# Column sums for a softmax: two column tiles of 64 with 512 columns, or four of 32 with 256

## The chip, the cores and the metric

The kernel runs on one core of one Trainium2 chip. Five engines work side by side there, each through its own list of instructions: TensorE (PE in the profile, with PEld for its weight loads), VectorE (DVE), ScalarE (ACT), GpSimd (POOL) and SyncE (SP), which here issues nearly all transfers. The metric is the time on the device in microseconds (us), lower is better; the time before is 1205.87 us, the median of three runs from 1204.80 to 1207.79.

## The reference

A block of a diffusion transformer: for two sequences of 1024 tokens with 256 features, all in float32, a layer norm, self-attention with 16 heads of 64, cross-attention to 77 tokens of context, a gated feed-forward, and then a second feed-forward with weights rounded to -1, 0, 1. The change touches the softmax of self-attention alone:

```python
def mha(xq, ctx, wq, wk, wv, wo, bo):
    b, sq, _ = xq.shape
    sk = ctx.shape[1]
    q = (xq @ wq).reshape(b, sq, H, DH).transpose(0, 2, 1, 3)
    k = (ctx @ wk).reshape(b, sk, H, DH).transpose(0, 2, 1, 3)
    v = (ctx @ wv).reshape(b, sk, H, DH).transpose(0, 2, 1, 3)
    scores = jnp.einsum('bhqd,bhkd->bhqk', q, k) / math.sqrt(DH)
    attn = jax.nn.softmax(scores, axis=-1)
    out = jnp.einsum('bhqk,bhkd->bhqd', attn, v)
    out = out.transpose(0, 2, 1, 3).reshape(b, sq, INNER)
    return out @ wo + bo
```

## The kernel before

Self-attention is cut into 32 units (NU = B * NP * 2): a unit is one sequence, one pair of heads and one half of the queries (512). Its scores are kept transposed, with keys on the 128 partitions and 2 x 512 queries of the two heads in the 1024 columns, in eight blocks of 128 keys (kb). So the softmax runs down the partitions: the maximum and the sum of a query are over partitions and over the eight blocks.

For each block, PE makes the scores in a tile of two PSUM banks (`scores`, L342, matmul L347), ACT copies them to SBUF (L927), and DVE keeps a running maximum (`running_max`, L357, L363). When the eight are done, DVE folds the maximum over the partitions (L366 to L385), a transfer writes it to DRAM and another spreads it to all partitions (`md`, `wide`, L386 and L387), and ACT places it in PSUM (`mb`, L391). Then each block is shifted by DVE (L400; one block by POOL, L395), exponentiated in place by ACT (L404), added on POOL into a running sum `pacc` (L411), and multiplied with the values on PE (`times_v`, L419).

The sums that the change rewrites come after this. `summed` (L448) lets PE multiply `pacc` by ones, which adds over the 128 partitions: `sums_by_ones` (L438) does it in two matmuls, one for each head, each of 512 columns, into the two halves of the partitions (two column tiles of 64; all 64 rows of a half hold the same numbers). The tile `tot` comes from the same two buffers of two banks each (`two_banks`, L53) as the scores. ACT copies it to SBUF as `rinv` (L454). `sums_packed` (L456) sends one row of each half to a row of 1024 in DRAM (`td`) and reads it back as 128 partitions of 8 numbers (`few`, L464). `inverted_packed` (L466) takes the reciprocal on DVE, writes it to DRAM and spreads it again over the 64 partitions of each half of `rinv` (L471). `normalised` (L480) multiplies the unit's output by it on POOL. The last two units take no part in the packing; their sums are inverted where they stand (`inverted`, L476), and the last unit's are added up block by block in PSUM (L969).

The order is written out by hand for PE, DVE, ACT and POOL (`manual_schedule`); SP's transfers are placed by the scheduler. The loop at L922 goes through slots, four to a unit (`q` = 0 to 3), two blocks in each. In a slot of unit u, PE does the two blocks of scores of u, then a piece of something else (projections, the product with wo, parts of cross-attention's weights; L281), and the values of older blocks, LAG = 7 slots behind. The sums of unit u - 3 stand at the end of slot q = 0 of unit u, their reciprocal at q = 1, the multiplication at q = 2. So on PE the sums are preceded by matmuls of the form 128 rows by 64 columns (L281 or L419) and followed by scores, which are 64 rows by 128 columns (L347).

Of the kernel before, what the change touches and what calls it, by code (L numbers as in the profile page):

```python
# [29 lines left out]
H, DH = 16, 64  # L30
# [13 lines left out]
def block_kernel(ctx: ExitStack, tc: tile.TileContext, a: dict, out: bass.AP):  # L44
    nc = tc.nc
    PSUM = bass.MemoryType.PSUM

    def g(name):
        return a["L0_" + name]
# [3 lines left out]
    def two_banks(name):  # L53
        return ps2.tile([P, 1024], FP, tag="s", name=name)
# [15 lines left out]
    ones = const.tile([P, P], FP, name="ones")  # L70
# [110 lines left out]
    NU = B * NP * 2  # L181
# [4 lines left out]
    with ExitStack() as sa:  # L186
# [9 lines left out]
        SQ = 32  # L196
        md = [dram.tile([1024], FP, name=f"md{u}") for u in range(NU)]
        td = [dram.tile([2, 1024], FP, name=f"td{u}") for u in range(NU)]
        sT, maccs, paccs, rinvs, tots, few = {}, {}, {}, {}, {}, {}
# [36 lines left out]
        for n in range(3):  # L236
            nc.scalar.dma_start(
                out=vec[4 * n : 4 * n + 4, :],
                in_=g(f"xcond_norm{n + 1}_b").rearrange("(o p) -> o p", p=P),
            )  # L240
        for c in range(DC):
            nc.scalar.dma_start(
                out=vec[28 + B * c : 28 + B * (c + 1), :],
                in_=a["cond_1024"][:, c * P : (c + 1) * P],
            )
        nc.scalar.dma_start(
            out=vec[12:28, :], in_=g("xcond_ff_b1").rearrange("(o p) -> o p", p=P)
# [190 lines left out]
        def sums_by_ones(tot, src, start, stop):  # L438
            for j in range(2):
                nc.tensor.matmul(  # L440
                    tot[j * DH : (j + 1) * DH, :512],
                    lhsT=ones[:, :DH],
                    rhs=src[:, j * 512 : (j + 1) * 512],
                    start=start,
                    stop=stop,
                )

        def summed(u):  # L448

            if u in paccs:  # L450
                tots[u] = two_banks("tot")
                sums_by_ones(tots[u], paccs.pop(u), True, True)
            rinvs[u] = p1.tile([P, 512], FP, tag="rinv", name="rinv")
            nc.scalar.copy(rinvs[u], tots.pop(u)[:, :512])  # L454

        def sums_packed(u):  # L456

            for j in range(2):
                nc.sync.dma_start(
                    out=td[u][0:1, j * 512 : (j + 1) * 512],  # L460
                    in_=rinvs[u][j * DH : j * DH + 1, :],
                )
            few[u] = small.tile([P, 8], FP, tag="few", name="few")
            nc.sync.dma_start(out=few[u], in_=td[u][0, :].rearrange("(p i) -> p i", i=8))  # L464

# [456 lines left out]
        for slot in range(NS + 12):  # L922
            u, q = slot // SLOTS, slot % SLOTS
# [4 lines left out]
            v, k = (slot - LAG + 1) // SLOTS, (slot - LAG + 1) % SLOTS  # L928
# [34 lines left out]
            w, k = (slot - LAG) // SLOTS, (slot - LAG) % SLOTS  # L963
# [9 lines left out]
            if slot == NS + 6:  # L973
                summed(NU - 1)
                for part in range(4):
                    inverted(NU - 1, part)
                normalised(NU - 1)
            elif q == 2 and 0 <= u - 3 < NU - 2:
                normalised(u - 3)
            elif slot == NS + 5:  # L980
                for part in range(4):
                    inverted(NU - 2, part)
                normalised(NU - 2)
            for job in extras.pop(slot, []):
                job[0](*job[1:])
            if slot in (NS + 7, NS + 8):
                n = slot - NS - 7
# [5 lines left out]
            if q == 0 and 0 <= u - 3 < NU - 1:  # L993
                summed(u - 3)
                if u - 3 < NU - 2:
                    sums_packed(u - 3)
# [41 lines left out]
        for name in ("w1", "w2"):  # L1038
# [4 lines left out]
            for i in range(2):  # L1043
                if name == "w1":
                    src = g("ffn_w1").rearrange("(c p) d -> p c d", p=P)[:, 4 * i : 4 * i + 4, :]
                    dst = raws[name][i].rearrange("p (c d) -> p c d", d=D)
                else:
                    src = g("ffn_w2")[i * P : (i + 1) * P, :]
# [173 lines left out]
    with (  # L1222
# [60 lines left out]
        for t in range(0, NT, 2):  # L1283
            i = t - TB
# [382 lines left out]
```

## Time and profile before

| What | Value |
|---|---|
| Median of three runs | 1205.87 us (1204.80 to 1207.79) |
| The profiled execution's own time | 1205.21 us |
| Its span, first to last instruction | 1203.4 us |
| Granted TensorE clock, mean over the span | 0.987 |
| Sums by ones, PE (L440) | 124 records of 592 ns |
| Copy of the sums, ACT (L454), 512 columns | 31, 585 ns in the middle |
| Scores' matmuls, PE (L347) | 1024 records, 258.1 us busy |
| Additions to pacc, POOL (L411) | 186 + 31, 2.37 us each |

The page of a profile gives busy time and counts of each engine over the span, the chain of work that ended last, and groups of instructions with the idle time before them and what ended it. A timeline lists instructions in order of time, those of one line merged: start, length, engine, line, operation, tiles written and read, shapes, number, and in brackets the idle time of the engine before it. For PE the shapes begin with rows*columns of the array that a matmul uses, and its lengths overlap, since matmuls are pipelined and their ends modelled: the time from start to start is the time that one takes. "A <- B" in a list of waits means that A's engine stood still until B was done; the numbers are total us, times, and the longest.

### The profile page before, as it was taken

The numbers are of one execution on the slowest core, as the hardware profiler recorded it, in microseconds if no ns is written. First come the engines' busy times: TensorE is split into PE (matmuls) and PEld (weight loads), VectorE is DVE, ScalarE is ACT, GpSimd is POOL, SyncE is SP. The second block draws the span as 40 slices with busy tenths as digits, with TensorE's granted clock in tenths as the row PEclk, the third lists the DMA queues.
The fourth block names the chain that finished last, engine by engine and source line by source line (L and its number), as shares of the span: only waits on it lengthen the run. The fifth ranks groups of instructions, "written<-read, shape, count | busy, mean of one in ns | idle before, by whom it ended". The sixth has DMA issues, their size and how long they took to land.

```text
span 1203.4 us, 16673 instructions
## 1 busy us (share of the span) xinstructions
PE 1166.8 (97%) x5885; PEld 576.5 (48%) x5885; DVE 946.1 (79%) x1398; ACT 814.6 (68%) x1032; POOL 809.6 (67%) x625
## 2 busy tenths in 40 slices
PE   8898999999999999999999999989999999999996
PEld 4342334334334343343433333346878766586684
DVE  4779789879888888988978988984767753568596
ACT  4788888888887887888889788751343341555365
POOL 5579888888888788879788989851425325433244
PEclk9999999999999999999999999999999999999996
DMA  7101212212122211311213112221020011000000
GB/s 229 36 30 42 76 53 64 69 52 68 45 78 60 64 56 54 88 33 54 65 48 108 58 45 88 77 65 36 1 66 20 1 62 35 1 18 10 9 10 27
DMA packets 65892, 63.23 MB, mean 53 GB/s; under 512 B 22875, under 2 KB 56149, under 8 KB 65297
## 3 DMA queue, kind: packets, MB, share of 16 engines
q1 hardware_dynamic: 65745, 62.15, 17.0%
q8 instruction: 46, 0.75, 0.3%
q14 instruction: 37, 0.30, 0.1%
q10 hardware_dynamic: 64, 0.02, 0.0%
HBM read 54.63 MB, written 7.52 MB: 52 GB/s over the span
## 4 chain that ended last, share of the span: by engine, by line
PE 81%; DVE 11%; ACT 4%; POOL 2%; issue 2%; DMA 0%; DVEq 0%; ACTq 0%; POOLq 0%
PE sc L347 16%; PE pav L419 16%; PE pp L281 9%; PE pu L1568 8%; PE sc L734 5%; PE po L801 5%; PE pv L281 4%; PE po L1594 4%; DVE macc L363 3%; DVE sT L400 3%; PE po L281 3%; PE tot L440 2%; ACT sT L927 2%; PE pu L1423 1%; PE po L1470 1%
## 5 line engine op out<-in xcount | busy, mean ns | idle before, releaser
L411 POOL TENSOR_TENSOR pacc<-pacc,sT 128x1024 f32<-128x1024 f32 x186 | 440.8, 2370 | 59.8 <-ACT sT L404 50.3
L363 DVE TENSOR_TENSOR macc<-macc,sc 128x1024 f32<-128x1024 f32 x192 | 233.8, 1218 | 77.7 <-ACT sT L927 66.1
L927 ACT COPY sT<-sc 128x1024 f32<-128x1024 f32 x256 | 247.5, 1015 | 51.4 <-PE sc L347 51.2
L404 ACT ACTIVATE sT<-sT 128x1024 f32<-128x1024 f32 x256 | 259.9, 1062 | 14.9 <-DVE sT L400 13.7
L347 PE MATMUL sc<-qT,kT 64*128 64x512 f32 x1024 | 258.1, 619 | 7.1 <-DVE macc L363 6.1
L400 DVE TENSOR_TENSOR sT<-sT,mb 128x1024 f32<-128x1024 f32 x225 | 261.8, 1206 | 2.8 <-ACT mb L391 2.8
L419 PE MATMUL pav<-sT,v 128*64 128x512 f32 x1024 | 250.0, 606 | 2.7 <-ACT sT L404 2.4
L347 PEld LDWEIGHTS sc<-qT,kT 64*128 64x128 f32 x1024 | 85.8, 185 | 158.3 <-DVE macc L363 60.5
L419 PEld LDWEIGHTS pav<-sT,v 128*64 128x64 f32 x1024 | 62.4, 136 | 151.1 <-issue 76.1
L1568 PE MATMUL pu<-h2T,ffw 128*128 128x512 f32 (+1 forms) x320 | 114.6, 509 | 0.0
L768 POOL TENSOR_TENSOR pr<-pr,t 128x616 f32<-128x616 f32 x32 | 39.2, 1225 | 104.1 <-DVE t L767 57.8
L411 POOL TENSOR_TENSOR pacc<-sT 128x1024 f32<-128x1024 f32 x31 | 73.8, 2381 | 46.0 <-ACT sT L404 46.0
L1568 PEld LDWEIGHTS pu<-h2T,ffw 128*128 128x128 f32 x320 | 59.5, 190 | 44.0 <-issue 39.9
L734 PE MATMUL sc<-G,h1T 128*128 128x308 f32 x256 | 74.0, 433 | 4.5 <-DVE pr L752 3.3
L801 PE MATMUL po<-U,pT 128*128 128x256 f32 (+1 forms) x320 | 74.4, 386 | 3.9 <-ACT pT L791 2.4
L395 POOL TENSOR_TENSOR sT<-sT,wide 128x1024 f32<-128x1024 f32 x31 | 73.7, 2378 | 2.1 <-DMA wide<-md 2.1
L801 PEld LDWEIGHTS po<-U,pT 128*128 128x128 f32 (+1 forms) x320 | 60.1, 193 | 13.4 <-ACT pT L791 3.2
L281 PE MATMUL pp<-h1T,wk 128*64 128x512 f32 x256 | 62.1, 607 | 0.9 <-ACT h1T L541 0.9
L281 PE MATMUL pv<-wv,h1T 128*64 128x256 f32 x512 | 60.9, 380 | 1.4 <-ACT qT L299 0.7
L281 PE MATMUL pp<-h1T,wq 128*64 128x512 f32 x256 | 60.5, 593 | 0.0
L734 PEld LDWEIGHTS sc<-G,h1T 128*128 128x128 f32 x256 | 47.6, 194 | 24.1 <-issue 9.5
L1586 DVE SCALAR_TENSOR_TENSOR gT<-pu,vecT,ge 128x512 f32<-128x512 f32 (+1 forms) x40 | 25.6, 641 | 42.0 <-ACT ge L1579 41.7
(183 smaller groups left out, 1541.2 us busy)
## 6 DMA issues: line engine op xcount, KB each, us to landing
wide<-md SPq DMA_DIRECT2D x32, 512.0 KB
rinv<-td SPq DMA_DIRECT2D x60, 128.0 KB
ffw<-in_L_xcond_ff_w_dram SPq DMA_DIRECT2D x3, 1024.0 KB
gd<-cw SPq DMA_DIRECT2D x32, 77.0 KB
ud<-cw SPq DMA_DIRECT2D x32, 77.0 KB
G<-gd SPq DMA_DIRECT2D x2, 1232.0 KB
wk<-in_L_xcond_attn_wk_dram SPq DMA_DIRECT2D x16, 128.0 KB
wq<-in_L_xcond_attn_wq_dram SPq DMA_DIRECT2D x16, 128.0 KB
```

The source lines that it names most:

```text
L281: nc.tensor.matmul(dst[half, :], lhsT=lhsT[:, half], rhs=rhs, start=start, stop=stop)
L347: nc.tensor.matmul(sc[:, j * 512 : (j + 1) * 512], lhsT=kTs[b, pair][rows, kb * P : (kb + 1) * P], rhs=qTs[b, pair][rows, qh * 512 : (qh + ...
L363: nc.vector.tensor_tensor(maccs[u], old, sc, ALU.max)
L395: nc.gpsimd.tensor_tensor(t, t, wides[u], ALU.subtract)
L400: nc.vector.tensor_tensor(sT[u, kb], sT[u, kb], mbs[u], ALU.subtract)
L404: nc.scalar.activation(t, t, AF.Exp)
L411: nc.gpsimd.tensor_tensor(paccs[u], old, t, ALU.add)
L419: nc.tensor.matmul(pavs[u][j * DH : (j + 1) * DH, :], lhsT=vs[b, pair // 2][:, kb, at : at + DH], rhs=sT[u, kb][:, j * 512 : (j + 1) * 512 ...
L734: nc.tensor.matmul(sc[:, i * 512 : i * 512 + HB * CTX], lhsT=hT[:, c, qb * P : (qb + 1) * P], rhs=Gs[b][:, c, at : at + HB * CTX], start=( ...
L801: nc.tensor.matmul(po[:, :D], lhsT=pT2s[n, part][:w, i * P : (i + 1) * P], rhs=Us[b][:w, half * 5 + c, :], start=(half + c == 0), stop=(ha ...
L927: nc.scalar.copy(sT[v, kb], sc)
L1568: nc.tensor.matmul(pu[:, k * 512 : k * 512 + n], lhsT=ffw1[c][:, at : at + P], rhs=hT[:, c, at0 : at0 + n], start=(c == 0), stop=(c == DC ...
```

## The change

For units 0 to 29 the sums are made by four matmuls instead of two. Each takes a quarter of the 1024 columns of `pacc` (256) and writes it to its own 32 partitions of `tot` (four column tiles of 32). The copy to `rinv` then has 256 columns instead of 512, and one transfer takes one row from each of the four groups of partitions (partitions 0, 32, 64 and 96) to the 1024 numbers in DRAM, where there were two transfers of 512. From there on nothing is different. Units 30 and 31 keep the old form.

```diff
+        def sums_in_quarters(tot, src):
+
+            for i in range(4):
+                nc.tensor.matmul(
+                    tot[i * SQ : (i + 1) * SQ, :256],
+                    lhsT=ones[:, :SQ],
+                    rhs=src[:, i * 256 : (i + 1) * 256],
+                    start=True,
+                    stop=True,
+                )
+
         def summed(u):
 
             if u in paccs:
                 tots[u] = two_banks("tot")
-                sums_by_ones(tots[u], paccs.pop(u), True, True)
+                if u < NU - 2:
+                    sums_in_quarters(tots[u], paccs.pop(u))
+                else:
+                    sums_by_ones(tots[u], paccs.pop(u), True, True)
             rinvs[u] = p1.tile([P, 512], FP, tag="rinv", name="rinv")
-            nc.scalar.copy(rinvs[u], tots.pop(u)[:, :512])
+            n = 256 if u < NU - 2 else 512
+            nc.scalar.copy(rinvs[u][:, :n], tots.pop(u)[:, :n])
 
         def sums_packed(u):
 
-            for j in range(2):
-                nc.sync.dma_start(
-                    out=td[u][0:1, j * 512 : (j + 1) * 512],
-                    in_=rinvs[u][j * DH : j * DH + 1, :],
-                )
+            nc.sync.dma_start(
+                out=td[u][0, :].rearrange("(i n) -> i n", n=256),
+                in_=rinvs[u].rearrange("(i k) n -> i k n", k=SQ)[:, 0, :256],
+            )
```

## The prediction

> **What bounds the kernel now.** I read the page's busy shares and its chain first, then a table by stage, then the order of time on PE around one set of sums, then DVE's, then the waits.
>
> ```profile
> PE 1166.8 (97%) x5885; PEld 576.5 (48%) x5885; DVE 946.1 (79%) x1398; ACT 814.6 (68%) x1032; POOL 809.6 (67%) x625
> PE 81%; DVE 11%; ACT 4%; POOL 2%; issue 2%; DMA 0%; DVEq 0%; ACTq 0%; POOLq 0%
> ```
>
> PE carries 81% of the chain that ended last. Self-attention runs from about 60 to 790 us; the table by stretch of its middle (PE, PEld, DVE, ACT, POOL busy) shows no idle PE, while DVE has 14% to spare and POOL 15%:
>
> ```profile
> 115.00:400.00 285.00, 284.77 (x1524) 109.85 (x1520) 244.31 (x275) 235.08 (x279) 241.21 (x108) 1.00 0.21 62
> ```
>
> PE's ends are modelled, so the busy share alone proves little; start-to-start times do. The timeline of PE near one set of sums (start, length, line, shapes, records):
>
> ```profile
> 442.23 1.90 PE L281 MATMUL pv<-wv,h1T 128*64 128x256 f32 x16
> 444.06 1.99 PE L347 MATMUL sc<-qT,kT 64*128 64x512 f32 x8
> 445.97 1.94 PE L419 MATMUL pav<-sT,v 128*64 128x512 f32 x8
> 447.74 1.89 PE L281 MATMUL pp<-h1T,wk 128*64 128x512 f32 x8
> 449.46 1.03 PE L440 MATMUL tot<-pacc,ones 128*64 128x512 f32 x4
> 450.42 1.99 PE L347 MATMUL sc<-qT,kT 64*128 64x512 f32 x8
> 452.33 1.27 PE L281 MATMUL pk<-cT,cw 128*64 128x154 f32 x16
> ```
>
> Every matmul is two records (31 sets of two sums appear as 124). From pp to tot, both 128*64, eight records take 1.72 us: 0.43 for two records of 512 columns. A full-width record of 512 columns alone also takes 0.43 (the chain has 66 of them in the feed-forward part in 28.38 us, first line of the next fence), so two column tiles do run side by side. A change of tile form shows as an excess over 0.43 a pair: tot to sc 0.96 - 0.86 = 0.10; sc to pav 1.91 - 1.72 = 0.19; pav to pp 1.77 - 1.72 = 0.05. So a change costs about 0.10 to drain, and then a first weight load that lies open: 0.09 for 128 columns (what sc's 0.19 has left after its own drain into pav), 0.05 for 64. Sixteen records of 256 columns take (1.83 - 0.10)/8 = 0.216 a pair.
>
> ```profile
> 982.95 28.38 PE pu L1568 x66
> ```
>
> Then who could hold PE back. The groups that PE itself waits for, and DVE's order of time in the same unit:
>
> ```profile
> PE sc L347 <- DVE macc L363: 6.1, 11, 1.6
> ```
>
> ```profile
> 452.98 2.53 DVE L363 TENSOR_TENSOR macc<-macc,sc 128x1024 f32<-128x1024 f32 x2
> 456.23 0.20 DVE L468 RECIPROCAL few<-few 128x8 f32<-128x8 f32 x1 [0.72 <-DMA few<-td]
> 459.24 2.55 DVE L363 TENSOR_TENSOR macc<-macc,sc 128x1024 f32<-128x1024 f32 x2 [2.81 <-ACT sT L927]
> 461.71 4.60 DVE L400 TENSOR_TENSOR sT<-sT,mb 128x1024 f32<-128x1024 f32 x4
> ```
>
> DVE stands 2.81 us some 10 us after the sums, until ACT has copied scores that PE has just made. So DVE follows PE anew in every unit; all waits of the scores' matmuls for the maximum are 6.1 us in the whole span.
>
> **What the skill says.** "TensorEngine Tiling (Array Packing)", Key Properties: a change of tiling mode, not of tile, drains the engine, and tiles run independently. The trace agrees for two tiles and gives the drain 0.10 us; four tiles of 32 columns it doesn't show. "TensorE: Matmul & The Clock Gate", Measured speedup vs the span model: three column tiles of 32 with 512 columns ran 2.38 times as fast as one after another, sixteen tiles (four by four) 10.6 times; nothing in this trace tells. The same page, LDWEIGHTS (loading the stationary operand): a load takes its columns over 1.2 GHz; that is 53 and 107 ns for 64 and 128, near the 50 and 90 seen open above, and gives an estimate of 27 ns for 32.
>
> **The change part by part.** 30 units (u below NU - 2) take the new form; u = 30 and 31 keep the old one.
>
> 1. PE removes two matmuls: 2 x 0.43 = 0.86 us a unit. It adds four matmuls of 256 columns in four column tiles. If the four run side by side, two passes of 0.215 = 0.43, plus 0.014 because two more records start 7 ns apart. Between pav/pp/pv/po (128*64) and the sums (128*32) a change of form appears that wasn't there: 0.093 drain (tile starts, to the ns, give 93) and 0.027 of weights. The drain into sc stays. Sum: 0.858 - 0.43 - 0.014 - 0.12 = 0.294 us saved. The new switch isn't in the trace; its bounds are nothing (if 64 to 32 columns is no change of mode) and 0.24 (the dearest seen, sc to pav with pav's weights); I take 0.12, the pattern of the other three. The four-deep packing is the one thing that decides; its bounds are under the rivals.
>
> 2. Which units keep it. In the slot after the sums the next scores find their bank free: the maximum that frees it ended 1.3 to 2.6 us before in 27 units, and POOL's last addition to pacc 11 us before the sums in all. Three units lose it: at 92.4 and 736.6 the maximum ended only 0.23 us before the next scores, and DVE-set waits follow at 98.9 and 743.1 with no DVE idle in between; at 781.6 the next matmul stood 3.3 us for DVE's pr (L752). Later waits (397, 536, 591, 685, 754, 777) come after DVE's stand of that unit, so DVE moves with PE. 27 x 0.294 = 7.9 us.
>
> 3. ACT's copy (L454) falls from 512 to 256 columns: 585 ns to about 370 (pT L791, 256 columns, takes 372), 0.215 x 30 = 6.4 us of ACT. ACT has 18% free in the stretch and waited for the sums (15.1 us in 27); worth nothing on the path. The tot bank comes back sooner: before, its copy ended 0.26 us before the second scores needed it; after, 0.5 of chain is gone against 0.3 of PE, so it isn't late.
>
> 4. SP: 30 transfers fewer, 0.25 us of issue and the 0.05 between each. The remaining one takes four rows of 1 KB from four partitions instead of two of 2 KB; its landing isn't in the trace. Bounds: 0.8 us sooner (0.5 from PE and ACT, 0.3 from SP), or 0.8 later if four rows land worse by that. Sooner removes DVE's 10.8 us of waiting for few (18 times), later doubles it; the 2.81 us stand right behind it swallows both. I take nothing.
>
> 5. Order: PE, ACT, DVE and POOL stand as before. On SP one thing moves: in the last unit the broadcast wide of u = 31 (issued 785.66) now stands behind td of u = 29, which waits for the rinv copy at 786.50 (ACT does it behind L761, which waits for DVE's pr). It is issued near 787.2, 1.5 us later. Its reader, ACT's mb copy at 792.27, is queued behind L761 at 791.64, so 5 us remain where such a broadcast's packets took 3. Nothing; up to 1.5 us if it were late.
>
> Sum: -7.9 against the profiled run's 1205.21 (span 1203.4 and 1.8 around it) is 1197.3; the median of the three runs is 0.66 above that run, so 1198.0.
>
> **The rivals.** (a) Forecast, 1198.0; own range with the switch at 0 to 0.24 and 26 to 30 units: 0.17 to 0.41 a unit, 4.5 to 12.4 us, 1193.5 to 1201.4.
> (b) Slower: fewer than four tiles run at once, in PE at the sums. The stream of eight pass-tiles of 0.215 then takes 0.86 with two at once, and with the switch and stagger each unit loses 0.86 + 0.134 - 0.858 = 0.136, 27 x 0.136 = 3.7: 1209.6. One at a time: 1.72, +1.0 a unit, 1233. It decides from a stream over 0.724 us. For it: the trace has no four; each matmul's two passes must be overtaken by three later matmuls, and only one such overtaking is seen. Against it: that one is perfect (a pair costs what one record costs), and the skill's table. Three at once: 0.645, 0.08 saved, 1203.7.
> (c) No change: DVE takes over. Scores at a unit's start find the maximum done only 0.05 to 0.75 us before, so a DVE that didn't move with PE would eat all but the first saving: 1205.5. Against it: DVE's stand of 0.7 to 3.1 us at 9 to 10 us after the sums in all units from 115 to 715.
>
> **Numbers.** (a) 0.77; (b) with two or one at once 0.13; three at once 0.05; (c) 0.05. What a measurement can tell from no change is 0.3%, 3.6 us (1202.3 to 1209.5): faster 0.77, same 0.10, slower 0.13. The range from 1193.5 to 1205.5 holds (a) but for its edges and the two quiet cases, and leaves out (b).
>
> **What would show it.** In the changed profile the tot group should have 240 records (30 x 4 x 2) of 128*32 beside the 4 old ones, four starting within 25 ns; first tot to sc near 0.57 us instead of 0.96, with about 0.10 more before it; the copy near 370 ns; units 0.3 us shorter, 23.9 to 23.6; the wait for few nearly gone. It is wrong if the tot starts lie 0.2 us apart one by one, if the sc wait for macc grows by more than some 2 us in total, or if the step from form to form costs over 0.4.

## The result and the profile after

The changed kernel takes 1198.72 us (median of five runs, 1196.84 to 1201.14) against 1205.87 for the kernel before in the same session (five runs, 1203.78 to 1207.79): a ratio of 0.9943, interval [0.9926, 0.9959]. The forecast was 1198.0. The profiled execution took 1200.08 us with a span of 1198.3. Lines from L476 on stand 14 lower down in the changed kernel: the new sums are L451, their copy L469, `td` L473, `few` L478.

The page of the kernel after, busy time by engine and the chain's shares:

```profile
PE 1160.1 (97%) x6005; PEld 573.0 (48%) x6005; DVE 945.3 (79%) x1398; ACT 808.9 (68%) x1032; POOL 810.6 (68%) x625
PE 79%; DVE 13%; ACT 5%; issue 2%; DMA 1%; POOL 1%; DVEq 0%; SPq 0%; ACTq 0%; POOLq 0%
```

PE has 120 records more and 6.7 us of busy time less; it still carries the chain, but DVE has gained two points in it. Two groups of the tile `tot`, kernel after (durations are least, middle, greatest, in ns):

```profile
L451 PE MATMUL tot<-pacc,ones x240: 379/391/403, 93.4 to 776.8; 128*32 128x256 f32 x120
L469 ACT COPY rinv<-tot x31: 353/373/589, 94.6 to 803.5; 128x256 f32<-128x256 f32 x30, 128x512 f32<-128x512 f32 x1
```

There are 240 records of the new form, and ACT's copy took 373 ns. (The part behind the last semicolon can be a sample of the shapes, with smaller counts.) The timeline of PE, kernel after, around the same set of sums as in the prediction:

```profile
444.63 1.89 PE L281 MATMUL pp<-h1T,wk 128*64 128x512 f32 x8
446.44 0.64 PE L451 MATMUL tot<-pacc,ones 128*32 128x256 f32 x8
447.01 1.99 PE L347 MATMUL sc<-qT,kT 64*128 64x512 f32 x8
```

From pp to tot it is now 1.81 us instead of 1.72, from tot to sc 0.57 instead of 0.96. To the ns, over the 24 sets after the first: the first four sums start at 0, 7, 13 and 20 ns, four more at 240 to 260, which are read as their second passes (each matmul is two records, and the trace doesn't number them), and the scores at 569 (before: 958). In front of them the gap from the last matmul rises by 100 ns. So 0.39 is won and 0.10 given back.

The unit is the interval from one set of sums to the next (us, from the starts of the first sum in each trace). One trace was kept of each kernel. Where nothing that bears on them was changed, the traces agree on most intervals to about 0.01, but not on those of sets 25, 27 and 29. So the intervals show more than the total does:

| Interval from set | 1 | 12 | 16 | 17 | 19 | 20 | 26 | first to last set | last set to end |
|---|---|---|---|---|---|---|---|---|---|
| before | 23.77 | 24.52 | 23.92 | 23.74 | 24.52 | 25.14 | 21.18 | 715.05 | 395.99 |
| after | 23.48 | 24.23 | 24.28 | 23.65 | 24.55 | 24.98 | 20.89 | 708.93 | 395.97 |

In 22 of 30 intervals the gain is 0.29 us. Intervals 0, 27 and 29 give nothing, as forecast. Intervals 16, 17, 19, 20 and 25 give little, nothing or a loss, which wasn't forecast. From the first to the last set, self-attention won 6.12 us in this pair of traces. The span won 5.1, because the first sums came 1.0 later; that start lay anywhere from 92.1 to 96.5 in the twelve traces.

One line of the list of waits (total us, times, longest), before:

```profile
DVE few L468 <- DMA few<-td: 10.8, 18, 0.8
```

After, with PE's own wait for the maximum, which was 6.1 us before:

```profile
DVE few L482 <- DMA few<-td: 19.1, 21, 2.6
PE sc L347 <- DVE macc L363: 6.7, 12, 1.8
```

PE's own wait for the maximum grew by only 0.6 us. DVE's wait for few, which was nearly to vanish, rose from 10.8 to 19.1. SP's waits for the landing of `md` rose as well. Before:

```profile
SPq L387 <- DMA md<-mrow: 12.8, 29, 1.0
```

After:

```profile
SPq L387 <- DMA md<-mrow: 21.2, 31, 2.5
```

SP issues `md`, `td`, then `wide` (L387, which waits until `md` has landed), then `few`. SP's timeline, kernel before, in the unit of the sums at 449.46:

```profile
450.85 0.31 SPq L386 DMA_DIRECT2D md<-mrow  x1
451.25 0.52 SPq L459 DMA_DIRECT2D td<-rinv  x2
452.24 0.34 SPq L387 DMA_DIRECT2D wide<-md  x1
452.74 0.34 SPq L464 DMA_DIRECT2D few<-td  x1
```

Kernel after, in the unit of the sums at 470.08 (set 16):

```profile
471.40 0.34 SPq L386 DMA_DIRECT2D md<-mrow  x1
471.84 0.52 SPq L473 DMA_DIRECT2D td<-rinv  x1
474.89 0.34 SPq L387 DMA_DIRECT2D wide<-md  x1
475.28 0.42 SPq L478 DMA_DIRECT2D few<-td  x1
```

DVE's timeline of the same kernel and unit:

```profile
478.88 0.20 DVE L482 RECIPROCAL few<-few 128x8 f32<-128x8 f32 x1 [2.22 <-DMA few<-td]
```

Two things are seen. First, the copy of the sums ended at about 471.2, but `td` was issued only behind `md`, which waits for DVE's `mrow`. Over the units, the middle time from the copy's end to `td` is 0.61 us, where it was 0.11; from the end of `td`'s issue to `few` it is 1.11 instead of 0.96. `few` goes out 3.3 us after the first sum in most units, as before: the half microsecond that PE and ACT won is lost again in SP's queue. This is why the wait did not vanish.

Second, here `wide` was issued 3.2 us after `md`'s issue ended instead of about 1. In the trace of transfers 15 of `md`'s 16 parts landed within 0.2 us of each other, and the last at 474.82. A packet (one piece of a transfer) of 16 KB on queue q8, which carries instructions, ran from 472.83 to 473.79, and the last two of `md`'s small packets start at 473.77 and 473.80, as it ends (which packets share an engine the trace doesn't say). There are 47 such packets in the span, one for about 256 of PE's instructions, so they are read as fetches of these, and that is 23.4 to 23.8 us apart here, a unit's length. So the meeting repeats: with the packets at 402.19, 425.58, 449.08 and 472.83, in sets 13 to 16, `few` goes out 1.3 to 1.9 us late. These four units make up some 7 of the 8.3 us by which the wait for few rose. DVE's stand later in the unit absorbs the delay in three of them. In the fourth the scores waited for the maximum near 488 and interval 16 lost its gain.

That loss hangs on tenths of a microsecond. Two other kernels below also have their `md` late in sets 13 to 16. In set 16 `wide` followed the end of `md`'s issue by 3.16 us in the kernel after and interval 16 is 24.28; by 2.98 with two transfers, and it is 23.95; by 2.70 with the later norm, and it is 23.63, the whole gain.

Intervals 17 and 20 are held by DVE. DVE and PE's weight loads, kernel after, 4.5 and 7.1 us after the sums at 494.36 (set 17):

```profile
498.90 2.54 DVE L363 TENSOR_TENSOR macc<-macc,sc 128x1024 f32<-128x1024 f32 x2
501.49 0.30 PEld L347 LDWEIGHTS sc<-qT,kT 64*128 64x128 f32 x4 [0.76 <-DVE macc L363]
```

The second of these two maxima ends at 501.43, 7.07 us after the first sum, and the scores that take its bank load their weights 0.06 later. Before, they loaded at 7.23 and their matmul followed at 7.42, so this wait lay hidden. DVE has no stand of more than 0.10 us from 1.7 us before these sums until this point, so the maximum doesn't come sooner when PE saves 0.39 us after the first sum; DVE's next stand, of 0.65 us, ends only at 8.35. Interval 20 is the same to 0.01 us (maximum 7.07, weights 7.12).

Intervals 27, 29 and the way from the last set to the end depend on the granted clock (the share of TensorE's full speed that it was allowed). The traces' records of the clock show stretches of 3.4 us at half speed, alone or two in a row. Interval 27 is 22.93 to 22.95 in the seven traces without one there, whatever the form of the sums, and 23.42 to 23.87 in the five with one. Interval 29 is 24.12 with none, 25.5 to 25.8 with one, 26.5 to 27.1 with two. The way to the end is 393.8 to 394.3 in the seven traces without and 395.7 to 396.0 in the five with one some 163 us after the last set. Before and after both have all three, so this pair is alike in it.

### The profile page after: what moved, and what is told of

Read it like the earlier page. It is cut to its first block, busy times and chain, and to the rows that moved or that the text cites. A ratio compares the mean times of both kernels' runs of the same rounds, so it can differ in the third digit from the quotient of the medians.

```text
span 1198.3 us, 16887 instructions
## 1 busy us (share of the span) xinstructions
PE 1160.1 (97%) x6005; PEld 573.0 (48%) x6005; DVE 945.3 (79%) x1398; ACT 808.9 (68%) x1032; POOL 810.6 (68%) x625
## 4 chain that ended last, share of the span: by engine, by line
PE 79%; DVE 13%; ACT 5%; issue 2%; DMA 1%; POOL 1%; DVEq 0%; SPq 0%; ACTq 0%; POOLq 0%
PE sc L347 16%; PE pav L419 15%; PE pp L281 9%; PE pu L1582 9%; PE sc L748 5%; PE po L815 5%; PE pv L281 4%; DVE macc L363 4%; PE po L1608 4%; DVE sT L400 4%; PE po L281 2%; ACT sT L941 2%; PE pu L1437 1%; PE tot L451 1%; PE po L1484 1%
## 5 line engine op out<-in xcount | busy, mean ns | idle before, releaser
L404 ACT ACTIVATE sT<-sT 128x1024 f32<-128x1024 f32 x256 | 260.0, 1062 | 15.9 <-DVE sT L400 14.6
```

The source lines that it names most:

```text
L404: nc.scalar.activation(t, t, AF.Exp)
```

## The experiments

Kernels that were timed together share the runs of the kernel before (medians): 1205.51 us for the form alone, one transfer, two transfers and bf16 in four tiles; 1206.05 for the fetches, the copy twice, bf16 in two tiles and the later norm; 1204.82 for the half copy and for the last one. Times are given as median and ratio to these, with the interval.

**The change of form alone.** The kernel before, with the two sums of 512 columns in column tiles of 32. The copy keeps its 512 columns, but covers the 64 partitions that hold sums.

```diff
+                nc.tensor.matmul(
+                    tot[j * SQ : (j + 1) * SQ, :512],
+                    lhsT=ones[:, :SQ],
+                    rhs=src[:, j * 512 : (j + 1) * 512],
...
-                sums_by_ones(tots[u], paccs.pop(u), True, True)
+                if u < NU - 2:
+                    sums_in_halves(tots[u], paccs.pop(u))
+                else:
+                    sums_by_ones(tots[u], paccs.pop(u), True, True)
...
-                    in_=rinvs[u][j * DH : j * DH + 1, :],
+                    in_=rinvs[u][j * SQ : j * SQ + 1, :],
```

> The kernel before with the form of the sums alone changed: still two matmuls of 512 columns, but each in a column tile of 32 instead of 64; copy of 512 columns and two transfers as before. If the stream on TensorE decides, the stream stays at 0.86 us and only the new change of form is paid: 0.12 us a unit in 27 units, +3.3 us against before (1209), first sums to next scores about 0.99 us and 0.09 more before it. If the gain of the change comes from the shorter copy and the single transfer, or if a change of form costs nothing, this kernel is equal to before within 1 us.

1206.96 us, ratio 1.0013 [1.0003, 1.0022]. 26 of the 30 intervals are 0.12 or 0.13 us longer than before: the price that the prediction took for the new switch. The total missed the expected 1209: the medians differ by 1.45, and the interval leaves 0.4 to 2.7, not 3.3. From the first to the last set the trace is 2.67 us longer; it would be 3.16 but for interval 27, which lacks the half-speed stretch that the trace of before has there. The group of `tot` of this kernel:

```profile
L451 PE MATMUL tot<-pacc,ones x120: 592/605/617, 92.4 to 784.9; 128*32 128x512 f32 x120
```

With the same columns as before and only the form new, the first sum starts 100 ns later behind the last matmul, its second pass comes at 453 ns instead of 429, and the scores at 983 instead of 958: 0.10 in front of the sums and 0.025 within them.

**One transfer instead of two, alone.** The kernel before, with one transfer of two rows.

```diff
-            for j in range(2):
-                nc.sync.dma_start(
-                    out=td[u][0:1, j * 512 : (j + 1) * 512],
-                    in_=rinvs[u][j * DH : j * DH + 1, :],
-                )
+            nc.sync.dma_start(
+                out=td[u][0, :].rearrange("(j n) -> j n", n=512),
+                in_=rinvs[u].rearrange("(j k) n -> j k n", k=DH)[:, 0, :],
+            )
```

> The kernel before with its two transfers of the sums packed into one of two rows of 2 KB; matmuls and copy as before. If TensorE decides, no change (within 1.5 us of before), whatever the wait for few does. The rival, that a shorter chain from the sums to the reciprocals is a part of the gain, wants 1 to 3 us less than before.

1205.69 us, ratio 0.9999 [0.9987, 1.001]. No interval moved by more than 0.04 up to set 24; the wait for few fell from 10.8 to 8.5 us and bought nothing that can be told. The rival's 1 to 3 us are excluded but for the least of them (the interval leaves at most 1.6).

**Two transfers in the changed kernel.** The opposite: the four rows in two transfers of two.

```diff
-            nc.sync.dma_start(
-                out=td[u][0, :].rearrange("(i n) -> i n", n=256),
-                in_=rinvs[u].rearrange("(i k) n -> i k n", k=SQ)[:, 0, :256],
-            )
+            for j in range(2):
+                nc.sync.dma_start(
+                    out=td[u][0, j * 512 : (j + 1) * 512].rearrange("(i n) -> i n", n=256),
+                    in_=rinvs[u].rearrange("(i k) n -> i k n", k=SQ)[
+                        2 * j : 2 * j + 2, 0, :256
+                    ],
+                )
```

> The changed kernel with two transfers of two rows each instead of one of four; matmuls and copy as in the changed kernel. If TensorE decides, it keeps the changed kernel's time: 7 us less than before, 1198 to 1200. If the single transfer is a part of the gain, it loses 1 to 3 of these. Second question: in the profile of the changed kernel four units in a row stood 2 us for few, because the write of the maximum landed late beside an instruction fetch. If this comes from the shape of the single transfer, it is gone here; if it comes from where TensorE's instruction fetches fall in a unit, it stays, since TensorE's instructions are the same.

1198.53 us, ratio 0.9935 [0.9916, 0.9953]: not to be told from the changed kernel. `td` still stands 0.61 us behind the copy, and the late parts of `md` stay in the same four units. The packing into one transfer is therefore no part of the gain that can be told.

**Shifting PE's instruction fetches.** The changed kernel with 8 instead of 24 of the transposes that only keep PE busy at the very start, so that all later fetches fall 32 instructions later.

```diff
-        for i in range(24):
+        for i in range(8):
             nc.tensor.transpose(pv[:, P : 2 * P], ident, ident)
```

> The changed kernel with 8 instead of 24 warm-up transposes on TensorE at the start: 32 instructions fewer before the first unit, so every later instruction fetch of TensorE falls about 2.9 us later in its unit (32 of 256 instructions of a unit of 23.5 us). If the late landings of the maximum's write at the 14th to 17th sums come from fetches that fall on it, they go, the wait for few falls from 19 to about 11 us, and the unit of 24.28 us becomes 23.63. If they come from the new transfer or from the data's way, they stay. In total 0 to 1 us less than the changed kernel, beside what the start itself gains or loses.

1200.49 us, ratio 0.9947 [0.9929, 0.9965]. Interval 16 is 23.63, the 0.29 that was missing, and interval 17 now has the loss: 24.04 instead of 23.65. SP's timeline in the unit that was late, and in one that wasn't:

```profile
472.90 0.34 SPq L386 DMA_DIRECT2D md<-mrow  x1
473.34 0.52 SPq L473 DMA_DIRECT2D td<-rinv  x1
474.33 0.34 SPq L387 DMA_DIRECT2D wide<-md  x1
...
497.10 0.34 SPq L386 DMA_DIRECT2D md<-mrow  x1
497.49 0.54 SPq L473 DMA_DIRECT2D td<-rinv  x1
500.12 0.34 SPq L387 DMA_DIRECT2D wide<-md  x1
```

The first `wide` leaves 0.5 us after `td`, the second 2.1; fetches now start at 477.32 and at 498.05. The lateness went with the fetches, so they are its cause. All twelve traces bear this out: in 21 units the last part of `md` landed 1.9 us or more after its issue ended (1.0 in most), each time 1.0 to 1.2 us after the end of such a packet; no `md` without one was later than 1.74. Not every meeting delays: packets that began about 1 us after `md`'s issue ended did so in some units and not in others. The total doesn't gain: the fetches now meet sets 17, 18 and 20, and interval 17 loses what 16 wins. So half of the forecast failed, that the lateness would be gone and the wait for few would fall to about 11 us (15.1).

**ACT's copy twice.** The changed kernel copies `tot` to `rinv` a second time.

```diff
-            nc.scalar.copy(rinvs[u][:, :n], tots.pop(u)[:, :n])
+            nc.scalar.copy(rinvs[u][:, :n], tots[u][:, :n])
+            if u < NU - 2:
+                nc.scalar.copy(rinvs[u][:, :n], tots[u][:, :n])
+            del tots[u]
```

> The changed kernel with ScalarE's copy of the sums (256 columns, 0.37 us) done twice: 0.37 us more of ScalarE in 30 units, more than the change took from it. If ScalarE's part is worth nothing, as forecast, the time is that of the changed kernel within 1.5 us. If the shorter copy is a part of the gain, 5 to 10 us of it are lost here.

1199.35 us, ratio 0.9935 [0.9919, 0.9952]; by time not to be told from the changed kernel. The intervals tell more: 23.59 instead of 23.48 in set 1, and 0.10 or 0.11 more in most. The waits of PE's weight loads for the copy, changed kernel:

```profile
PEld sc L347 <- ACT rinv L469: 8.4, 29, 0.6
```

This kernel:

```profile
PEld sc L347 <- ACT rinv L471: 20.1, 29, 1.0
```

The second scores after the sums take `tot`'s banks. In the changed kernel the copy ends 1.08 us after the first sum starts, their weights load at 1.13, and their matmul comes at 1.53. A second copy ends at 1.48, the load starts at 1.53 and lies open, and the next matmul is 0.10 later. So the single copy has less than 0.40 us to spare: 0.3 by an estimate from these two numbers (0.40 later, 0.10 lost).

**Sums in bf16, four tiles.** The changed kernel, where POOL's last addition writes `pacc` in bf16 and PE multiplies by ones in bf16. This rounds the sum over the eight blocks to bf16 before it is added over the partitions.

```diff
-                nc.gpsimd.tensor_tensor(paccs[u], old, t, ALU.add)
+                if kb == TB - 1 and u < NU - 2:
+                    last = paccs[u].bitcast(BF)[:, :1024]
+                    nc.gpsimd.tensor_tensor(last, old, t, ALU.add)
+                    paccs[u] = last
+                else:
+                    nc.gpsimd.tensor_tensor(paccs[u], old, t, ALU.add)
...
-                    lhsT=ones[:, :SQ],
+                    lhsT=ones_bf,
```

> The changed kernel, but the last addition of the running sum writes bfloat16, and the sums by ones run on bfloat16 (the sums are taken from rounded numbers; nothing else differs). A bfloat16 matmul should be one record instead of two and stream a column in half the time: four tiles of 256 columns in about 0.11 us instead of 0.43. If TensorE decides, 0.32 us more is saved a unit, 0.29 to 0.32 x 26 = 8 us beyond the changed kernel: about 1191. If DVE is near to taking over, less than half of this: 1195 or more, with more waits of scores for macc.

1190.08 us, ratio 0.9864 [0.9847, 0.9882]. The group of `tot` of this kernel:

```profile
L458 PE MATMUL tot<-pacc,ones_bf x120: 282/283/283, 92.2 to 766.1; 128*32 128x256 bf16 x120
```

One record instead of two for each sum; first sum to scores is 0.22 us instead of 0.57, and most intervals lie 0.64 below before's. Intervals 17, 19, 20 and 21 stand where the changed kernel has them (23.65, 24.55, 24.98, 24.23 against 24.22), although 0.35 more was won on PE. So in these four something else than PE sets the length. In 17 and 20 it is the same maximum, which still ends 7.08 and 7.07 us after the first sum; the scores' matmul there now starts 0.20 us after PE's last work. In 21 DVE stood 0.46 instead of 0.10 us between two maxima some 17 us after the sums.

**Sums in bf16, the old two tiles.** The kernel before with bf16 sums: the same addition, and two matmuls of 64 rows and 512 columns.

```diff
...
-                sums_by_ones(tots[u], paccs.pop(u), True, True)
+                sums_by_ones(
+                    tots[u], paccs.pop(u), True, True, ones_bf if u < NU - 2 else ones
+                )
```

> The kernel before with the last addition of the running sum written as bfloat16 and the two sums of 512 columns taken on bfloat16 in the old form of 64 columns, copy and transfers as before (the sums are taken from rounded numbers). From the prices so far: a stream of 512 bfloat16 columns 0.215 us instead of 0.86 and no new change of form, so 0.64 us saved a unit, the same as four tiles of 32 with bfloat16 (0.11 and 0.12 for the form): 1190 within 1.5 us. If the four-tile form itself is worth more than its stream, or the longer copy and second transfer cost anything, it stays above 1192.

1193.03 us, ratio 0.9887 [0.9868, 0.9907]: a miss by some 3 us. Most intervals lie only 0.48 below before's (23.29 in set 1). PE reached the scores 0.64 us sooner as computed (first sum to scores 0.32 instead of 0.96), but the second scores lost 0.06 there and 0.10 after: the copy of 512 columns ends at 1.29 us, and the matmul that needs its bank was due at 1.28. It started at 1.34.

**The same, with the bank given back sooner.** ACT copies only the first 256 columns out of `tot` and fills the other half of `rinv` from that copy; half of the sums are left out.

```diff
-            nc.scalar.copy(rinvs[u], tots.pop(u)[:, :512])
+            if u < NU - 2:
+                nc.scalar.copy(rinvs[u][:, :256], tots.pop(u)[:, :256])
+                nc.scalar.copy(rinvs[u][:, 256:], rinvs[u][:, :256])
+            else:
+                nc.scalar.copy(rinvs[u], tots.pop(u)[:, :512])
```

> The kernel of bf16 sums in the old two tiles of 64, but ACT copies only the first 256 columns of tot to rinv, and fills the other half of rinv from that copy: half of the sums are left out, so that this is a measurement of the bank's release and not the whole computation. There the full copy of 512 columns ends 1.290 us after the first sum's start, and the second pair of scores, which takes that bank, starts at 1.343 as an open form step, where 1.279 without was due. Theory: the copy holds that bank, and this is all that parts two bf16 tiles from four (0.48 against 0.64 us a unit). Then the first copy ends by about 1.07, the second pair of scores starts 0.963 us after the first as in the kernel before, PE's wait for rinv falls from 19.7 to 14 us or less, the units lie 0.64 under before's, and the time is 1190 plus or minus 1. Rival: the second transfer on SP or the two tiles themselves cost it: units stay 0.48 under before's and the time at 1193 plus or minus 1.

1190.89 us, ratio 0.9882 [0.9862, 0.9903]. The waits of PE's weight loads for the copy, two tiles with the whole copy:

```profile
PEld sc L349 <- ACT rinv L463: 19.7, 29, 1.0
```

With half of it:

```profile
PEld sc L349 <- ACT rinv L464: 13.5, 29, 0.8
```

Most intervals are 0.64 below before's (23.13 in set 1), and the same as with the four bf16 tiles to 0.01, and the second scores start at 1.278 us. In bf16 four tiles win nothing on PE over two (first sum to scores 0.22 and 0.10 more in front of it, against 0.32): what they bring is the shorter copy.

**The second part of norm 1 a slot later.** In the changed kernel ACT stood, near interval 19, for a value of POOL's that it needs for the norm of the next stage; the job is put off by one slot.

```diff
-            at_slot(extras, first + 9 + t + t // 4 * 8, lambda t=t: norms[1, 0].centred(t))
+            at_slot(extras, first + 10 + t + t // 4 * 8, lambda t=t: norms[1, 0].centred(t))
```

> The changed kernel with the centring of the second norm of the first sequence one slot later. In the changed kernel ScalarE stood 2.3 us there for GpSimd's root (nm), the unit at the 20th sums took 24.55 us and kept none of its 0.29 us. If that wait is what holds the unit, it falls to 23.6 to 24.2 us, and 0.3 to 1 us is won in all. If VectorE is what holds it, it stays at 24.5.

1196.45 us, ratio 0.9912 [0.9895, 0.9929]. Interval 19 fell from 24.55 to 23.48. ACT's timeline in the changed kernel:

```profile
546.06 2.01 ACT L404 ACTIVATE sT<-sT 128x1024 f32<-128x1024 f32 x2
550.39 0.60 ACT L146 ACTIVATE xn<-r_sb,nm,r 128x256 f32<-128x256 f32 x1 [2.32 <-POOL nm L140]
550.90 0.56 ACT L301 COPY kT<-pp 128x512 f32<-128x512 f32 x1
551.37 1.93 ACT L941 COPY sT<-sc 128x1024 f32<-128x1024 f32 x2
```

In this kernel, which is 1.6 us ahead there:

```profile
544.44 2.01 ACT L404 ACTIVATE sT<-sT 128x1024 f32<-128x1024 f32 x2
547.11 0.59 ACT L301 COPY kT<-pp 128x512 f32<-128x512 f32 x1 [0.65 <-PE pp L281]
548.22 1.93 ACT L941 COPY sT<-sc 128x1024 f32<-128x1024 f32 x2 [0.53 <-POOL r L138]
```

ACT stood 2.32 us in front of L146 with kT's copy and two copies of scores queued behind it. Without that job there, the scores' copies come 1.5 us sooner after L404 (3.8 us after its start instead of 5.3). Interval 17 stays at 23.65 and 20 at 24.91: this job isn't their limit. By the medians the total fell by more than the forecast 0.3 to 1 us, but this job accounts for 1.07 alone: of the 4.0 us that the trace lies below the changed kernel's from the first to the last set, 0.65 stand in interval 16, and 2.2 in 27 and 29, where this trace has no half-speed stretch.

**Both: bf16 sums in four tiles and the later norm.** The two edits above together.

> The kernel of the bf16 sums in four tiles with the second part of norm 1 one slot later. If the stand of 2.32 us of ACT for POOL's nm is what holds the unit of the sums at about 541 (24.55 in before, after and with bf16 sums alone; 23.48 with the later slot alone), that unit falls to 23.1 to 23.5 here and the two gains add: 1187.5 to 1189.0. If another wait stands at the same place once the sums are shorter, that unit stays at 23.5 or more, or the next ones rise above 23.65, 24.98 and 24.23, and the time stays within 0.7 of 1190.1.

1189.64 us, ratio 0.9873 [0.9854, 0.9891]. Interval 19 is 23.13, as forecast. From the first to the last set the trace fell from 700.34 us with bf16 alone to 697.89, of which interval 19 is 1.42 and interval 29, with one half-speed stretch instead of two, 0.96. The total doesn't show it and missed its range: against that run the first sums came 1.4 us later, and the way from the last set to the end took 395.66 us instead of 393.75, where eight matmuls of cross-attention (`po<-U,pT`) followed each other at 0.43 us instead of 0.22. The clock's record says why. This stretch of the trace (busy us of PE, PEld, DVE, ACT, POOL; then the granted clock):

```profile
954.00:957.40 3.40, 3.40 (x12) 2.47 (x11) 2.15 (x4) 0.72 (x1) 1.30 (x2) 0.50 0.02 5
```

With bf16 alone the clock is 1.00 there. Two microseconds of this kind hide a gain of this size. The median is the lowest of all, but against the kernel before of its own session the ratio is no better than that of bf16 alone (0.9864): the two can't be told apart.

## Why the forecast held, point by point

**Step 1, PE's account: held to 0.005 us.** It said 0.294 a unit; 22 intervals lost 0.289 in the mean. The stream: four matmuls start within 20 ns and the second pass follows at 0.240, the 0.216 of a single pass of 256 columns and the 0.025 of weights that the form alone costs. So four tiles of 32 did run side by side, which the trace of before couldn't show; rival (b) is out. The switch was taken at 0.12 by the pattern of three others, between bounds of 0 and 0.24; the form alone cost 0.12 (0.10 in front, 0.025 within). The Trainium skill, "TensorEngine Tiling (Array Packing)", Key Properties, says that changing the mode and not the tile drains the engine: 64 to 32 columns is such a change here, at 100 ns more in front of the first sum. One reading was a little low: the open load of 128 columns, taken at 0.09, is 0.105 (from the first to the second pass of the scores behind the sums it is 534 ns, against 429 where the load is hidden); nothing rested on it. The same list says that different tiles work in parallel: seen here for four.

**Step 2, which units keep it: the term of the sum that was mis-sized.** It gave 27 units and 7.9 us; self-attention won 6.12 in the traces. The three units that it struck out (sets 0, 27, 29) indeed gave nothing. It missed intervals 16, 17, 19, 20 and 25, which kept +0.36, -0.09, +0.03, -0.16 and +0.05 instead of -0.29 each. The method was at fault: it asked whether DVE stands idle somewhere in each unit, and took that to mean that DVE moves with PE. That holds for what comes after the stand alone. In 17 and 20 the scores 7.1 us after the sums take a bank whose maximum DVE finishes at 7.07, and its next stand ends only at 8.35 us: DVE runs through from before the sums and moves with them, but not with what PE saves after them. Rival (c), DVE takes over, was written off for the whole span and holds for these two. The other three were shown to hang on other things: in 16 a late landing of `md`, in 19 ACT's stand for POOL. In 25 it is a stand of 0.46 us between two maxima that DVE otherwise takes 0.10 apart: the interval is 22.93 with it (22.94 with the fetches moved) and 22.59 without it (two transfers). It comes in five traces, one of them with the old sums, and what causes it isn't shown.

**Step 3, ACT's copy at nothing: held, with less room than thought.** The copy fell from 585 to 373 ns. Doubling it cost 0.11 us a unit, so the release of the bank is less than 0.4 us from being the limit; once the sums are in bf16 and two tiles, the long copy costs 0.16 a unit.

**Step 4, SP: right in the time, wrong in the wait.** It allowed `few` 0.8 us sooner or later, took nothing on the time, and wrote that the wait for few would be nearly gone. The wait rose instead: 19.1 us against 10.8. `td` didn't leave SP when the copy ended, because `md` stands ahead of it in SP's queue and waits for DVE. Before, the copy ended as `md`'s issue was ending, so in the middle unit the order cost 0.11 us (in eight units, where `md` came later, already 0.6 to 0.8); a copy that ends 0.58 us sooner meets it. That takes back 0.50 us, and the landing took 0.15 longer. With one transfer of two rows in the kernel before, the landing takes 1.08 against 0.96 for the second of two, and 1.10 with two transfers of two rows in the changed kernel, so it isn't four rows that make it late. Beyond that, the fetches of PE's instructions, which the forecast had not on its list at all, held back `md` in four units, and most of the rise is theirs. That the time hardly felt it rests on DVE's later stand, as the forecast said; in interval 16 the stand was too short.

**Step 5, the last `wide` behind `td`: held.** `wide` was issued at 782.35, 2.9 us after the end of `md`'s issue instead of 1.1, and its reader, ACT's `mb` copy, came at 787.17 right behind the instruction ahead of it, without a wait for `wide`. Interval 29, where this falls, is 25.76 against 25.80. With the later norm, where interval 29 had no half-speed stretch, this copy waited 0.33 us for `wide`: the room is smaller than the 5 us that were taken.

The sum came out at 1198.0 against 1198.72 by a right price for each unit and a count that was five units too high; the ratio's interval leaves 4.9 to 8.9 us, and doesn't tell 6.1 from 7.9.

## What to carry to other kernels

Price an edit on a full PE by the start-to-start times in its own trace (stream, drain, open weight load), and then test the count of places that keep the gain: another engine's idle time makes safe only the waits that come after it, and only if what ends it moves with PE. A wait that lies between the saving and that idle time has to be checked for itself. When a step gets faster, look at what stands ahead of its successor in that queue, since a transfer that becomes ready sooner may only wait longer behind one that waits for something else. Packing sums of this kind into column tiles can pay by the time that the result's bank is held as well as by PE's stream: here the stream in fp32, and the bank alone in bf16, where two tiles were as good on PE as four. And before a difference of 2 us between two traces is explained, their granted clocks should be compared stretch by stretch.

## What was unexpected of the hardware

- The second pass of an fp32 matmul is overtaken by the first passes of matmuls on other column tiles that stand behind it in the program, if the eight records are read as above: the second pass of the first sum starts at 240 ns, the first passes of the other three at 7, 13 and 20. In bf16, with one record each, the four start within 10 ns.
- A bf16 sum of four tiles saves more than a pass: first sum to scores fell from 0.569 to 0.223 us. 0.240 of this is the pass that falls away, 0.096 that the way from the last sum's start to the scores is shorter (0.213 instead of 0.309), and the rest the closer starts. The one pass that is left is faster too: with 512 bf16 columns in two tiles that way is 0.309, as with 256 fp32 columns.
- Fetches of PE's instructions, 16 KB each and 0.9 to 1.3 us long where they met such a transfer, held up the last of 16 parts of a write of 4 KB by 0.7 to 2.1 us. They come once in about 256 instructions of PE, so a loop of about that length meets them at the same place again and again.
- At the end of self-attention and in cross-attention the granted clock fell to half for 3.4 us at a time, at about the same places, but in some traces and not in others. The one in cross-attention cost some 2 us. What starts such a stretch isn't shown.
